# One operation moved from VectorE into ScalarE's root, and a new order of all engines, in a recurrent block on one core

## The chip, the cores and the metric

The kernel runs on one core of a Trainium2 chip. The metric is the time of one execution in device microseconds, from the first to the last work of the core. The engines are TensorE (PE: matmuls; PEld is its weight load), VectorE (DVE), ScalarE (ACT), GpSimd (POOL) and SyncE (SP), which issues most of the transfers. Each works through its own list in order and waits on semaphores for the others.

## The reference

The input `x` has 8 sequences of 1024 tokens with 256 channels, in float32. The block normalizes each token and adds two branches to it:

```python
xn = _layernorm(x)
x = x + hawk(xn) + ffn(xn)

# hawk: 384 hidden channels
gate = einsum('bsd,hd->bsh', xn, Wg);  u = einsum('bsd,hd->bsh', xn, Wi)
y = causal_conv4(u, conv_w) + conv_b                    # per channel
ig = sigmoid(einsum('bsh,gh->bsg', y, lru_Wi) + lru_bi)
rg = sigmoid(einsum('bsh,gh->bsg', y, lru_Wg) + lru_bg)
alpha = exp(-8.0 * softplus(lam) * rg)
beta = sqrt(1.0 - alpha ** 2 + 1e-06)
xbeta = beta * ig * y
h[t] = alpha[t] * h[t-1] + xbeta[t]                     # a scan over the tokens
hawk = einsum('bsh,dh->bsd', gelu(gate) * h, Wo)

# ffn: a token mix, then
r = sigmoid(xr @ W_r);  k = square(relu(xk @ W_k));  ffn = r * (k @ W_v)
```

`xr` and `xk` mix each token with the one before it, by channel.

## The kernel before

The kernel goes through the 8 sequences one after the other; a hidden tile is `[128 channels, 3 chunks m, 1024 tokens]`, so an operation on one chunk is 128x1024, and a half is 512 tokens (L or R). All data is float32.

Most of the products are done by a scheme that saves one in eight: `Group` (L569) makes a 2x2 block product of seven products (11 for `o`), from sums of weight blocks (`weight_sum`, POOL, once at the start) and sums of token halves (`token_sum`, POOL, L1024). Its steps are named after the family: `u0`, `u1`, `u2` (the 768 outputs of `Wi` and `Wg`), `k`, `r`, `v` and `o`. `k mm 0` to `k mm 6` are the seven products (PE; `product` at L533, two matmul instructions of 128x512 each, or `product_by_token` at L539, eight of 128x128); `seed` copies bank A to a new bank B and `five` bank C to SBUF (ACT, L589, L593); `fork_c` and `fork_d` add B to what was copied (DVE, L596, L605); `evict` and `late` take results out. Product 0 goes to bank A, which `seed` must copy before product 2 (by token: 3) adds to it. Product 4 adds the token sum 1 of the family, which is made by `token_sum k 2`. In the first sequence `u0` is made by plain products instead, in four quarters of the tokens for each of two blocks (`u0_0 quarter`, L668, four instructions of 128x256), so that work can begin with the first tokens; its input `xnT` comes by PE transposes and four copies (`early_put`, ACT, L1246).

The gates `rg` and `ig` use a 3x3 scheme with 15 products each (`rg p11`, ...), from sums of halves of `y` (`form`, DVE, L816) and of weights (`gate_weight`, POOL, L858, once). `keep` and `copy` are copies of banks (ACT, L727, L724), `join` adds a bank and a kept half (DVE, L735), and `evict` takes the tanh of a bank into `tr` (for `rg`) or `ti` (for `ig`) (ACT, L739). A sigmoid is made of the tanh of half the argument, so that a factor 0.5 is left over for later.

The steps around the change work on one chunk `m`:

- `decay(m)` (ACT, L1135): `tr` becomes a = exp(rate * tr + rate). `rate` comes from the parameters by small steps `constant 0` to `constant 18`, the last of them at L498 on DVE.
- `decay_square(m)` (ACT, L1138): `q` = a a.
- `decay_rest(m)` (DVE, L1141): `q` = 1 - a a.
- `beta(m)` (ACT, L1144): `q` = sqrt(q + 1e-6).
- `gated_input(m)` (DVE, L1148): `ti` = (ti + 1) * y; `scaled_input(m)` (DVE, L1151): `ti` = 0.5 * ti * q.
- `recur(m)` (DVE, L1156): the scan, by halves; `gated_state` (DVE, L1160): gelu(gate) times the state, which the products with `Wo` read (`o mm`, and for the last sequence `own o_product` and `own o_tile`, L1051).

In the sequences 0 to 6 `decay`, `decay_square` and `decay_rest` stand in the sequence's own part of the order and the rest in the next one's; the last sequence does all of it for itself (`own ...`). Other steps that are named below: `normalize` (ACT, L970, for the sequence after), `deviation` (its root, L953), `stats` (DVE, L946, L950), `mix_before` and `mix` (ACT, L1035, and DVE, L1041: the token mix), `add_x` (a transfer issued by POOL that adds `x` to the output tile, L1078), `halve v` (POOL, L514).

ScalarE holds the tables of a set of functions at a time. The trace shows a load (ACT_TABLE_LOAD) before the root, the exponential, the tanh and the gelu when another kind came before; exp and tanh share a set, gelu and tanh as well.

The order of every engine is written out: `at(f, ...)` adds a step under its name, with the position that `PLACES` holds for that name ("first", "second", "middle" and "last" sequence) plus the sequence's entry of `BASES`. At the end all steps are sorted by position and issued, each on its engine. The positions are in the unit of microseconds, but only their order has an effect; data dependences and semaphores follow from the order.

Of the kernel before, what the change touches and what calls it, by code (L numbers as in the profile page):

```python
# [9 lines left out]
AF = mybir.ActivationFunctionType  # L10
ALU = mybir.AluOpType
# [7 lines left out]
BETA_EPS = 1e-6  # L19
# [17 lines left out]
        "early_transposes 1": -8.6439, "u0_0 quarter 1 0": -8.0543, "early weight_sum u 2": -3.8020,  # L37
        "early_put 1": -3.0538, "early normalize 4 1": -0.3355, "early weight_sum k 0": -0.0898,
        "early weight_sum k 1": -0.0893, "early weight_sum r 2": -0.0060,
        "early weight_sum k 2": 0.6225, "early deviation 6 2": 0.8567, "early weight_sum r 0": 1.1454,  # L40
        "early normalize_on_vector 5": 1.2994, "u0_0 quarter 0 0": 1.2999, "early_transposes 2": 1.2999,
        "u0_0 quarter 0 1": 1.3004, "early inverse 6 2": 1.4202, "early normalize_on_vector 7": 1.4207,
        "early normalize 6 1": 1.4212, "early gate_weight 18": 1.5352, "early weight_sum u 0": 1.7246,
        "early weight_sum u 1": 1.7251, "early_put 2": 1.7885, "early gate_weight 0": 1.8328,
        "early parameters": 1.9171, "early_transposes 3": 1.9259, "early_put 3": 1.9264,
        "early mix_before k 1": 1.9269, "u1 mm 0": 3.1720, "early token_sum x 0": 3.5163,
        "u0_0 quarter 1 1": 3.5290, "early weight_sum u 3": 3.6691, "u2 mm 0": 3.7112,
        "early mix k 1": 3.8314, "early constant 0": 4.0632, "early token_sum x 1": 4.4256,
        "early mix_before k 0": 5.9712, "early mix k 0": 6.0616, "early load 0 8": 7.4642,
        "early mix_before r 0": 8.3295, "early mix r 0": 8.3300, "u2 seed": 8.6340,  # L50
        "u0_0 evict 1 0": 8.7097, "u0_0 evict 0 0": 8.7413, "early token_sum x 2": 9.4143,
        "early token_sum k 0": 10.1772, "second stats 5 1": 10.6110, "early token_sum r 0": 10.8667,
        "second stats 4 1": 11.3491, "u0_0 quarter 1 2": 11.4875, "u0_0 quarter 1 3": 11.4879,
        "u0_0 evict 1 1": 11.4885, "u2 mm 1": 11.8761, "u1 mm 1": 12.0652, "second stats 1 1": 12.2744,
        "early token_sum k 1": 12.2953, "u1 seed": 12.3010, "u2 five": 12.6356,
        "early constant 1": 12.6580, "u1 mm 2": 13.0964, "u1 evict A 0 0": 13.0969,
        "early constant 2": 13.2671, "second stats 3 1": 13.9558, "second stats 6 1": 13.9907,
        "u2 mm 3": 14.2992, "conv_first 1": 14.5919, "second stats 7 1": 14.6574,
        "second stats 2 1": 15.0552, "early weight_sum k 3": 15.5297, "second stats 0 1": 15.5372,
        "conv_rest 1 1": 15.5372, "u2 mm 2": 16.0627, "early mix_before r 1": 16.3697,  # L60
        "k mm 0": 16.3737, "k seed": 16.3742, "k mm 2": 16.3747, "k mm 1": 16.4858,
        "k evict A 0 0": 16.4931, "u0_0 quarter 0 2": 16.8650, "early token_sum k 3": 16.9641,
        "k five": 17.1660, "early constant 3": 17.1999, "conv_rest 1 2": 17.7117, "deviation": 17.8286,
        "u0_0 quarter 0 3": 18.2151, "early token_sum k 2": 18.5156, "k mm 3": 19.5026,
        "k fork_c": 20.0768, "early constant 4": 20.1410, "early constant 5": 20.1415,
        "early constant 6": 20.1420, "u0_0 evict 0 1": 20.2772, "u2 evict A 0 0": 20.2868,
        "early halve v": 20.6806, "inverse 0 8": 21.3608, "normalize 1 1": 21.3613,
        "early constant 7": 21.5110, "early mix r 1": 21.5785, "early weight_sum r 1": 22.0990,
        "normalize 6 1": 22.6887, "r mm 0": 23.1799, "r seed": 23.1804, "k mm 4": 23.9848,
        "r mm 3": 24.1395, "k fork_d": 24.1400, "early constant 8": 24.1585, "u2 fork_c": 24.2562,  # L70
        "u1 mm 3": 24.5089, "normalize 7 1": 24.8151, "u1 five": 24.9788,
        "early token_sum r 1": 25.1316, "r evict A 0 0": 25.2098, "conv_first 0": 25.4504,
        "normalize 2 1": 25.4982, "early gate_weight 11": 25.6372, "k mm 5": 25.7409,
        "early token_sum r 2": 26.1668, "k mm 6": 26.1955, "r mm 2": 26.1986, "r mm 1": 26.6667,
        "conv_rest 1 3": 27.0060, "conv_rest 0 1": 28.4200, "u1 fork_c": 28.6675,
        "conv_rest 0 2": 28.9892, "u1 mm 4": 29.5016, "u1 mm 5": 29.5176, "k evict B 1 0": 29.6818,
        "k evict C 0 1": 29.6820, "k square 0": 29.6823, "normalize 5 1": 29.8290, "r five": 29.8586,
        "u1 evict C 0 1": 30.1053, "u2 mm 5": 30.8282, "normalize 4 1": 30.9791,
        "transposes 1 1": 30.9796, "early token_sum x 3": 30.9835, "k late": 31.4107,
        "early constant 9": 31.9860, "early weight_sum v 0": 32.0816, "u1 fork_d": 32.0871,  # L80
        "r fork_c": 32.0872, "early constant 10": 32.0935, "conv_rest 0 3": 32.0938,
        "early constant 11": 32.0940, "early weight_sum o 0": 32.1222, "early gate_weight 17": 32.3477,
        "r mm 4": 33.0834, "form 0": 33.3300, "form 1": 33.3305, "u2 mm 4": 33.8429,
        "v_product 0": 33.8429, "early weight_sum r 3": 34.1459, "transposes 0 1": 34.1807,
        "normalize 0 1": 34.3885, "k square 1": 35.0468, "conv_first 2": 35.0517,
        "u2 evict C 0 1": 35.0972, "put_transposed 1 1": 35.1766, "u1 mm 6": 35.7392,
        "early gate_weight 19": 36.6572, "v_product 4": 37.0114, "conv_rest 2 1": 37.0336,
        "early gate_weight 2": 37.1069, "early token_sum r 3": 37.4370, "r fork_d": 37.5271,
        "r late": 37.5276, "early constant 12": 37.5345, "u2 fork_d": 37.7650, "u2 mm 6": 38.3899,
        "r mm 6": 38.4971, "conv_rest 2 2": 38.6946, "early constant 13": 39.4021,  # L90
        "early gate_weight 7": 39.4190, "conv_rest 2 3": 39.4739, "early gate_weight 1": 39.4739,
        "early gate_weight 12": 39.4744, "put_transposed 0 1": 39.6428, "u1 evict B 1 0": 39.6492,
        "normalize 3 1": 39.6727, "transposes 1 0": 39.6732, "put_transposed 1 0": 39.6737,
        "r mm 5": 39.6869, "form 2": 39.7379, "early weight_sum v 2": 39.7441,
        "early gate_weight 4": 39.8463, "early gate_weight 8": 40.0476, "transposes 0 0": 40.1660,
        "put_transposed 0 0": 40.4633, "v_product 2": 40.7467, "r evict C 0 1": 40.8812,
        "u2 evict B 1 0": 40.9052, "u1 late": 40.9351, "r evict B 1 0": 41.0098, "form 3": 41.2098,
        "form 4": 43.0821, "ig p11": 43.0826, "rg p11": 43.7513, "load_for_squares": 44.8161,
        "rg copy B": 45.3918, "v_product 6": 45.3923, "rg p0": 45.3923, "token_sum x 0": 45.7012,
        "value 4": 45.7514, "rg p4": 46.4712, "value 2": 46.7711, "early gate_weight 5": 46.9214,  # L100
        "form 8": 47.2752, "early gate_weight 13": 47.3300, "form 5": 48.1910, "ig copy B": 48.2529,
        "mix_before r 1": 48.2544, "rg keep 14": 48.2575, "rg keep 10": 48.7892,
        "early gate_weight 9": 49.4059, "early gate_weight 10": 49.7857, "ig p4": 50.0465,
        "ig keep 10": 50.2130, "early gate_weight 15": 50.5880, "mix_before k 0": 50.5982,
        "form 6": 51.2676, "value 6": 51.6062, "form 7": 51.6063, "early gate_weight 6": 51.9650,
        "form 9": 52.1153, "stats 2 1": 52.1945, "mix_before r 0": 53.6127, "ig p0": 53.8491,
        "rg p3": 53.9727, "stats 6 1": 54.4985, "stats 4 1": 54.5807, "mix_before k 1": 54.6938,
        "rg p10": 55.4065, "early gate_weight 16": 55.5289, "ig p3": 55.6292, "ig keep 14": 55.8307,
        "ig p10": 55.8312, "rg keep 13": 55.8456, "rg p7": 55.9304, "mix r 0": 55.9576,
        "early constant 14": 56.1814, "early gate_weight 14": 56.5499, "rg copy E": 57.4426,  # L110
        "ig keep 13": 57.6010, "rg join G": 57.9749, "rg p2": 57.9754, "rg keep 8": 57.9834,
# [1350 lines left out]
```

## Time and profile before

| | us |
| --- | --- |
| median of 3 runs (lowest to highest) | 621.52 (620.99 to 622.68) |
| profiled execution, its time | 621.6 |
| its span, first to last instruction | 619.8 |
| busy: PE, DVE, ACT, POOL | 598.8, 569.1, 489.7, 281.9 |
| L1141 on DVE, 24 instructions | 19.1 |
| L1144 on ACT, 24 roots | 27.5 |
| table loads on ACT, 39, each | 1.28 |

The granted TensorE clock is 1.00 throughout. Busy times of PE count each matmul to its modelled end, and matmuls that follow each other overlap: in a steady run two instructions of 128x512 take 0.86 us, and one of them is listed with 0.595. So PE's idle time, not its busy share, tells what is to be had.

### The profile page before, as it was taken

Reading aid. Unit: us, or ns where it says so; the run is one execution under the profiler, and the core shown is the slowest. Engines: PE = TensorE matmul, PEld = TensorE weight load, DVE = VectorE, ACT = ScalarE, POOL = GpSimd, SP = SyncE. Lnnn points to the kernel's source line nnn. Section 1 sums busy time; section 2 is a strip of 40 time slices with the busy share of each in tenths; the row PEclk is TensorE's granted clock in tenths of the full one; section 3 lists DMA queues with packets and bytes.
Section 4 is the critical chain, followed back from the end, with each engine's and each line's share of the span. In section 5 each row is a group of like instructions: output and inputs, shape, how many; then the busy total and the mean of one; then the engine's idle time right before and its main releaser. Section 6 shows DMA issues by size and latency. Waiting matters only on the chain.

```text
span 619.8 us, 7495 instructions
## 1 busy us (share of the span) xinstructions
PE 598.8 (97%) x2491; PEld 358.6 (58%) x2491; DVE 569.1 (92%) x772; ACT 489.7 (79%) x730; POOL 281.9 (45%) x205
## 2 busy tenths in 40 slices
PE   8888999999999999999999999999999999999997
PEld 4456434684357844586446954569445774555576
DVE  5999889998999988999899998999989997798896
ACT  4985799928998489974999479993899839995890
POOL 4998592245616363362823546154552618110010
PEclk9999999999999999999999999999999999999999
DMA  7203004053300434017040250403430020400053
GB/s 272 68 2 69 1 0 68 0 113 92 55 13 3 122 81 68 1 27 175 4 69 2 61 143 6 63 0 98 106 55 14 22 82 33 68 2 1 0 85 120
DMA packets 35478, 35.10 MB, mean 57 GB/s; under 512 B 2800, under 2 KB 34928, under 8 KB 35440
## 3 DMA queue, kind: packets, MB, share of 16 engines
q1 hardware_dynamic: 26416, 25.63, 15.4%
q0 software_dynamic: 8320, 8.39, 9.1%
q10 hardware_dynamic: 704, 0.60, 0.3%
q8 instruction: 20, 0.33, 0.2%
q14 instruction: 18, 0.15, 0.1%
HBM read 19.94 MB, written 8.39 MB: 46 GB/s over the span
## 4 chain that ended last, share of the span: by engine, by line
PE 72%; DVE 16%; ACT 8%; issue 3%; POOL 1%; DVEq 0%; ACTq 0%; POOLq 0%
PE bank L533 52%; PE bank L539 17%; DVE y L1124 5%; PE bank L1051 2%; DVE xk L1041 1%; DVE bank L596 1%; PE bank L1214 1%; DVE u L816 1%; POOL q L1024 1%; DVE xk L1001 1%; ACT q L1144 1%; ACT xk L1035 1%; POOL xsum L1024 1%; DVE side L914 1%; ACT bank L724 1%
## 5 line engine op out<-in xcount | busy, mean ns | idle before, releaser
L1124 DVE SCALAR_TENSOR_TENSOR y<-u,par,y 128x1024 f32<-128x1024 f32 x72 | 96.3, 1360 | 0.8 <-ACT y L1115 0.7
L533 PE MATMUL bank<-u,gate_w 128*128 128x512 f32 x192 | 92.6, 595 | 1.8 <-ACT side L896 1.0
L533 PE MATMUL bank<-y,gate_w 128*128 128x512 f32 x160 | 78.7, 595 | 1.1 <-ACT bank L724 1.1
L533 PE MATMUL bank<-xsum,sum_u 128*128 128x512 f32 x138 | 69.8, 597 | 1.3 <-DVE bank L596 1.2
L533 PE MATMUL bank<-ysum,gate_w 128*128 128x512 f32 x128 | 64.8, 595 | 2.1 <-ACT ti L727 1.6
L533 PEld LDWEIGHTS bank<-u,gate_w 128*128 128x128 f32 x192 | 34.9, 189 | 42.1 <-issue 32.9
L533 PEld LDWEIGHTS bank<-y,gate_w 128*128 128x128 f32 x160 | 29.7, 189 | 39.9 <-issue 28.2
L1035 ACT ACTIVATE xk<-xnT,mu_rest 128x1024 f32<-128x1024 f32 x16 | 18.4, 1148 | 41.6 <-DMA xnT<-xk 24.6
L1024 POOL TENSOR_TENSOR xsum<-xnT 128x512 f32<-128x512 f32 x16 | 22.7, 1433 | 56.7 <-DMA xnT<-xk 32.1
L533 PE MATMUL bank<-xnT,w_u 128*128 128x512 f32 x92 | 47.1, 593 | 0.5 <-ACT bank L589 0.5
L1024 POOL TENSOR_TENSOR q<-g 128x512 f32<-128x512 f32 x12 | 20.1, 1672 | 60.2 <-DVE g L1160 60.2
L724 ACT COPY bank<-bank 128x512 f32<-128x512 f32 x48 | 27.8, 582 | 23.8 <-PE bank L533 20.0
L1024 POOL TENSOR_TENSOR q<-g,q 128x512 f32<-128x512 f32 x12 | 25.3, 2104 | 46.1 <-DVE g L1160 30.5
L533 PEld LDWEIGHTS bank<-ysum,gate_w 128*128 128x128 f32 x128 | 23.7, 189 | 34.0 <-issue 19.5
L596 DVE TENSOR_TENSOR bank<-bank,five 128x512 f32<-128x512 f32 x52 | 35.0, 688 | 6.5 <-PE bank L539 4.3
L533 PEld LDWEIGHTS bank<-xsum,sum_u 128*128 128x128 f32 x138 | 24.1, 190 | 26.9 <-issue 19.4
L593 ACT COPY five<-bank 128x512 f32<-128x512 f32 x52 | 30.7, 590 | 10.1 <-PE bank L539 9.5
L970 ACT ACTIVATE xt<-xt,mv,std 128x256 f32<-128x256 f32 x60 | 35.2, 597 | 2.3 <-DVE mv L961 2.3
L539 PE MATMUL bank<-w_o,g 128*128 128x128 f32 x288 | 36.9, 275 | 0.0
L539 PEld LDWEIGHTS bank<-w_o,g 128*128 128x128 f32 x288 | 35.0, 192 | 2.9 <-issue 2.9
L1151 DVE SCALAR_TENSOR_TENSOR ti<-ti,q 128x1024 f32<-128x1024 f32 (+1 forms) x25 | 29.3, 1173 | 3.4 <-ACT q L1144 3.3
L589 ACT COPY bank<-bank 128x512 f32<-128x512 f32 x52 | 30.6, 589 | 2.2 <-PE bank L539 1.3
(187 smaller groups left out, 1589.1 us busy)
## 6 DMA issues: line engine op xcount, KB each, us to landing
side<-in_x_dram POOLq DMA_DIRECT2D x8, 1024.0 KB, 9.4
xt<-in_x_dram SPq DMA_DIRECT2D x28, 256.0 KB, 4.9
xnT<-xk SPq DMA_DIRECT2D x96, 64.0 KB, 2.0
out_dram<-side SPq DMA_DIRECT2D x12, 512.0 KB, 3.3
xt<-in_x_dram SPq DMA_DIRECT2D x1, 1024.0 KB, 5.6
out_dram<-side SPq DMA_DIRECT2D x4, 256.0 KB, 2.2
out_dram<-side SPq DMA_DIRECT2D x6, 128.0 KB, 1.8
q<-in_lru_wg_dram SPq DMA_DIRECT2D x1, 576.0 KB, 6.1
```

Of the source, the lines that this page charges most:

```text
L533: nc.tensor.matmul(banks[b], weight, tokens, start=start, stop=True, skip_group_check=True)
L539: nc.tensor.matmul(banks[b][:, p], tokens[:, p], weight, start=start and j == 0, stop=True, skip_group_check=True,)
L589: nc.scalar.copy(banks[bank["B"]], banks[bank["A"]])
L593: nc.scalar.copy(held["five"], banks[bank["C"]])
L596: nc.vector.tensor_tensor(banks[bank["C"]], banks[bank["B"]], held["five"], ALU.add)
L724: nc.scalar.copy(banks[bank[new]], banks[bank[key]])
L970: nc.scalar.activation(xa, xa, AF.Identity, bias=m, scale=r)
L1024: nc.gpsimd.tensor_tensor(dst[o], a, b, ALU.subtract)
L1035: nc.scalar.activation(mixes[which][:, c, :], xnT[:, c, X0 - 1 : X0 - 1 + S], AF.Copy, scale=mu_rest[:, n : n + 1])
L1051: nc.tensor.matmul(banks[b][:, j * D : (j + 1) * D], lhs[:, c, (t + j) * P : (t + j + 1) * P], families[w][:, c, :], start=(j == 0 and c = ...
L1124: nc.vector.scalar_tensor_tensor(y[:, m, :], u[:, m, k : k + S], column(COL_CONV_W + k * HC + m), y[:, m, :], ALU.mult, ALU.add,)
L1151: nc.vector.scalar_tensor_tensor(ti[:, m, p], ti[:, m, p], 0.5, q[:, m, p], ALU.mult, ALU.mult)
```

## The change

`decay_rest` goes, 24 instructions on DVE. `beta` takes a a itself: its scale is -(10^6)/2^20 and its bias (10^6 + 1)/2^20, which makes it sqrt((1 + 1e-6 - a a) * 10^6/2^20), that is the root of before times 1000/1024. `scaled_input` takes 0.512 for 0.5, which makes up for it. `PLACES` and `BASES` are new as a whole (the names are the same but for `decay_rest`), so every engine has a new order in all sequences.

```diff
-BETA_EPS = 1e-6
...
-BASES = [9.828, 71.0849, 152.108, 224.215, 296.322, 368.429, 440.537, 512.644]
+BASES = [10.9113, 57.2608, 149.2927, 221.3999, 293.5071, 365.6143, 437.7215, 511.5455]
...
-    beta_eps = fixed("beta_eps", [1])
+    beta_one = fixed("beta_one", [1])
...
-    def decay_rest(m):
-        nc.vector.tensor_scalar(q[:, m, :], q[:, m, :], -1.0, 1.0, ALU.mult, ALU.add)
-
     def beta(m):
-        nc.scalar.activation(q[:, m, :], q[:, m, :], AF.Sqrt, bias=beta_eps)
+
+        nc.scalar.activation(q[:, m, :], q[:, m, :], AF.Sqrt, bias=beta_one, scale=-(10**6) / 2**20)
...
     def scaled_input(m, p=slice(0, S)):
-        nc.vector.scalar_tensor_tensor(ti[:, m, p], ti[:, m, p], 0.5, q[:, m, p], ALU.mult, ALU.mult)
+        nc.vector.scalar_tensor_tensor(ti[:, m, p], ti[:, m, p], 0.512, q[:, m, p], ALU.mult, ALU.mult)
...
-        nc.gpsimd.memset(beta_eps, BETA_EPS)
+        nc.gpsimd.memset(beta_one, (10**6 + 1) / 2**20)
...
                 at(decay_square, m)
-                at(decay_rest, m)
```

The tables of positions are long; these are the stretches of the orders that they give which the prediction speaks of ("x 2" is `token_sum x 2`, "ws u 0" is `weight_sum u 0`, "q 1 0" is `u0_0 quarter 1 0`):

| | before | after |
| --- | --- | --- |
| PE, first sequence, from the second transposes | transposes 1, q 1 0, q 0 0, transposes 2, q 0 1, transposes 3, u1 mm 0, q 1 1, u2 mm 0, q 1 2, q 1 3, u2 mm 1, u1 mm 1, u1 mm 2, u2 mm 3, u2 mm 2, k mm 0, k mm 2, k mm 1, q 0 2, q 0 3, k mm 3, r mm 0, k mm 4, r mm 3, u1 mm 3, k mm 5, k mm 6, r mm 2, r mm 1 | q 0 0, q 1 0, transposes 1, 2, 3, q 1 2, q 0 2, q 0 3, q 1 1, q 0 1, u1 mm 1, u2 mm 0, q 1 3, u1 mm 0, k mm 0, u1 mm 3, u2 mm 2, k mm 1, u1 mm 2, u2 mm 3, k mm 2, u1 mm 5, r mm 0, u2 mm 1, k mm 3, u1 mm 4, u2 mm 4, u2 mm 5, transposes 1 0 (next sequence), u1 mm 6, k mm 4, k mm 5, r mm 1, r mm 3 |
| POOL, first sequence | ws u 2, k 0, k 1, r 2, k 2, r 0, u 0, u 1, gate_weight 0, x 0, ws u 3, x 1, x 2, k 0, r 0, k 1, ws k 3, k 3, k 2, halve v | ws u 0, u 2, r 0, u 1, r 2, k 2, r 1, k 0, gate_weight 1, 17, x 2, x 0, x 1, x 3, k 0, ws u 3, k 1, ws k 1, ws r 3, r 0, ws k 3, halve v, r 1, k 3, k 2, r 2 |
| ACT, first sequence | constant 1 (Exp), ..., deviation (root), u0_0 evict, u2 evict A (gelu), two normalize, r seed | deviation (root), u1 evict A, constant 1 (Exp), ..., u2 evict A (gelu), r seed |
| ACT, end of the first sequence | decay 0, rg copy F, decay_square 0, ig evict E, ig keep 8, ig copy F | rg copy F, ig keep 8, u0 five, ig evict G, ig copy F, decay 0, decay_square 0 |
| ACT, end of the last sequence | own beta 1, rg evict A, ig evict A, own decay 2, own decay_square 2, ig evict F, own beta 2 | own beta 1, rg evict A, ig evict A, own decay 2, own decay_square 2, own beta 2, ig evict F |
| DVE, end of the last sequence | gated_input 2 L, decay_rest 2, gated_input 2 R, ..., then behind the root: scaled_input 2 L, recur 2 L, gated_state 2 L, scaled_input 2 R, add_hawk 4, recur 2 R, add_hawk 2, gated_state 2 R | gated_input 2 L, ..., then behind the root: scaled_input 2 L, recur 2 L, gated_state 2 L, gated_input 2 R, scaled_input 2 R, recur 2 R, gated_state 2 R, add_hawk 4 |

## The prediction

> **What bounds the kernel now.** I read the busy times first, then the same by stage, then the waits of PE in the timeline, then the last 25 us on ACT and DVE.
>
> ```profile
> PE 598.8 (97%) x2491; PEld 358.6 (58%) x2491; DVE 569.1 (92%) x772; ACT 489.7 (79%) x730; POOL 281.9 (45%) x205
> ```
>
> ```profile
> 0.00:30.00 30.00, 25.06 (x86) 13.83 (x87) 22.60 (x55) 20.20 (x33) 21.61 (x29) 1.00 0.51 175
> 30.00:81.00 51.00, 45.05 (x170) 25.80 (x169) 45.48 (x66) 37.59 (x60) 39.75 (x37) 1.00 0.10 22
> 81.00:153.00 72.00, 68.61 (x306) 41.97 (x305) 67.61 (x87) 56.49 (x87) 32.87 (x23) 1.00 0.27 59
> 225.00:297.00 72.00, 71.47 (x314) 43.30 (x313) 68.48 (x89) 58.25 (x88) 32.06 (x21) 1.00 0.27 59
> 560.00:620.00 60.00, 54.94 (x213) 35.54 (x211) 49.90 (x68) 37.06 (x50) 4.08 (x3) 1.00 0.23 53
> ```
>
> The columns are the window, its length, then busy time and count on PE, PEld, DVE, ACT and POOL. PE is the bound: no matmul is added or removed, so only its idle time can be won, 21 us of the span in all. Of it 4.9 + 6.0 lie before 81 us and 3.4 in the second sequence; from 153 to 560 the windows add up to 1.8 us; the last window has 5.1, mostly behind the last matmul. So DVE's 92% hides behind PE almost everywhere, and the question is what the new order does at the two ends.
>
> ```profile
> 26.03 1.13 PE L533 MATMUL bank<-xk,w_k 128*128 128x512 f32 x2 [1.45 <-ACT bank L589]
> ...
> 34.80 1.16 PE L539 MATMUL bank<-w_r,xr 128*128 128x128 f32 x8 [1.62 <-ACT bank L589]
> ...
> 79.41 1.98 PE L533 MATMUL bank<-y,gate_w 128*128 128x512 f32 x4 [1.14 <-ACT bank L724]
> ...
> 168.85 1.10 PE L533 MATMUL bank<-xsum,sum_u 128*128 128x512 f32 x2 [0.42 <-DVE bank L596]
> ...
> 607.83 8.90 PE L1051 MATMUL bank<-w_o,g 128*128 128x256 f32 x40 [1.07 <-DVE g L1160]
> ```
>
> In brackets stands PE's idle time before each row and what ended it.
>
> **The step that goes.**
>
> ```profile
> L1141 DVE TENSOR_SCALAR q<-q 128x1024 f32<-128x1024 f32 x24 | 19.1, 798 | 2.6 <-ACT q L1138 1.9
> ```
>
> 24 instructions, 19.1 us of DVE, 2.0 to 2.8 per sequence. The median is 692 ns; one took 3.22 us:
>
> ```profile
> 162.96 1.54 POOL L1078 DMA_DIRECT2D side<-in_x_dram  x1
> ...
> 163.15 3.82 DVE L1141 TENSOR_SCALAR q<-q 128x1024 f32<-128x1024 f32 x2
> ```
>
> It stood beside POOL's issue of the `add_x` transfer; DVE came 2.5 us late to `u0 fork_c`, and PE waited the 0.42 us shown at 168.85. That goes: -0.4 (none if the new order puts another wait there; -1.1 if the 0.7 us that the waits give to the same line in the second sequence went too). Elsewhere PE's work hides the step; in the steady stretch I take -0.3 of the 1.8 us idle. The bounds are -1.8, and +2.0 if the new order opens waits there (153 to 225 has 0.95 idle, the next window 0.53: 0.4 more in each of five sequences). The cover that makes these 17 us worth nothing is PE itself.
> The Trainium skill ("SBUF — State Buffer", on the shared port pair) says that a one-source VectorE operation in a two-port mode and a GpSimd operation exclude each other for a whole instruction. The long row fits. By that rule every removed step would also free POOL, by an estimate 24 x 0.69 = 17 us, and the sum would be the same as long as POOL, 45% busy, isn't what PE waits for; the trace shows one long step in 24, and I count one.
>
> **What ScalarE takes on.** Nothing in number: the root has a bias from a tile already (24 x 1150 ns); the scale is a constant. Bounds: 1150 and, with a scale from a tile too, `decay`'s 1252; I take 1150, the same function and shape. The high end would put 3 x 0.10 = 0.3 us on the tail, the rest is hidden.
>
> **The start.** Here the order decides. Take a matmul step of 128x512 as a piece of 0.86 us (two instructions; the chain of waits has 34 of them in 14.68 us at 139.24). PE had done 14 pieces behind the transposes (6 quarters of `u0_0`, 8 steps) at 24.4, then waited 1.45: `k mm 2` stands right behind `k mm 0` and needs `k seed` on ACT. At 34.80 `r mm 3` waits for `r seed`, behind two table loads on ACT (28.66 and 30.74, 1.28 each). In the new list five steps stand between `k mm 0` and `k mm 2`, ten between `r mm 0` and `r mm 3`, and the Exp of `constant 1` comes after `deviation`, so one of the table loads goes. Both waits go. What is late next? POOL:
>
> ```profile
> 17.26 2.27 POOL L1024 TENSOR_TENSOR xsum<-xnT,xsum 128x512 f32<-128x512 f32 x1
> ...
> 28.00 2.25 POOL L1024 TENSOR_TENSOR xk<-xk 128x512 f32<-128x512 f32 x1
> ```
>
> The second row is `token_sum k 2`, done at 30.2; `k mm 4` needs it. In the new queue of POOL there stand ahead of and with it, from 8.34 on: three wide and five narrow weight sums and two gate weights (3 x 1.0 + 5 x 0.46 + 2 x 0.75 = 6.8, to 15.1), ten token sums, four more weight sums and `halve v` (1.0 + 3 x 0.45 + 2.47 = 4.8). The eight token sums from 15.05 to 30.25 took 1.26 to 2.27, mean 1.76: `k 2` ends at 15.1 + 17.6 + 4.8 = 37.5 (32.6 with all at 1.27, 42.4 with all at 2.25). PE on its side: the transposed input is whole at 14.4 (the four copies follow each other on ACT; before, 15.0), five quarters to 18.7, then seven pieces, 14 done at 24.7, then 11 pieces, `r mm 0` (0.9) and a transpose step (0.45) to 35.5. So `k mm 4` starts at 37.5, POOL the later. Before, as much was done at 39.9 (the thirteenth piece after the fourteen ended at 40.3; less 0.4, as one of mine is a transpose). The term is 37.5 - 39.9 = -2.4, from -4.4 (PE ready at 35.5 sets it) to +2.5 (42.4). I take the mean row, since both kinds come in the same stretch.
>
> **The decay rate.**
>
> ```profile
> 76.34 1.28 ACT L1135 ACT_TABLE_LOAD   x1 [1.70 <-DVE rate L498]
> ```
>
> `decay 0` waited for the last of the small constants on DVE, with two copies of the gate banks queued behind it on ACT; PE's 1.14 at 79.41 is that. In the new list `decay 0` comes behind these copies. What PE then meets isn't shown: 0 to -1.1, I take half, -0.5. The other waits up to 168 us (0.5 to 1.5 each, on ACT, DVE and POOL) I leave as they are: they are as likely to move as to go.
>
> **The tail.**
>
> ```profile
> 601.93 0.67 ACT L739 ACTIVATE ti<-bank,half_b 128x512 f32<-128x512 f32 x1
> 602.62 1.28 ACT L1144 ACT_TABLE_LOAD   x1
> 603.92 1.15 ACT L1144 ACTIVATE q<-q,beta_eps 128x1024 f32<-128x1024 f32 x1
> ...
> 602.06 0.69 DVE L1141 TENSOR_SCALAR q<-q 128x1024 f32<-128x1024 f32 x1
> ...
> 605.10 0.69 DVE L1151 SCALAR_TENSOR_TENSOR ti<-ti,q 128x512 f32<-128x512 f32 x1 [0.54 <-ACT q L1144]
> ```
>
> ACT runs without a gap from 576.6 to 605.1 and sets the last root. The removed step at 602.06 ended at 602.75, inside the table load: worth nothing. But the new list puts `ig evict F` (first row) behind the last root, which so comes 0.6 us earlier. Its price: one more table load (1.28) and the tanh (0.67) behind the root, 1.95, beside DVE's left half (scale 0.69, scan 1.22, gate 0.69 = 2.6); then `gated_input 2 R` (0.67) joins DVE's right half: 0.67 + 0.68 + 1.28 + 0.68 = 3.3 against PE's 16 matmuls x 0.216 = 3.5. Both fit, by 0.65 and 0.2. Gain -0.6, at most the 1.07 that PE waits; +0.7 if the right half isn't covered.
> Against this move speaks the Trainium skill ("ScalarE: Activation LUTs", What ACT_TABLE_LOAD costs), with about 2.66 us per switch, a drain included. The trace shows 1.28 to the start of the root; by the page's figure the left half would no longer cover load and tanh (an estimate: 3.3 against 2.6), and 0.7 would be lost.
>
> **Sum.** -0.4 - 0.3 - 2.4 - 0.5 - 0.6 = -4.2, from the profiled execution's 621.6 (span 619.8 and 1.8 around it): 617.4. The median of the runs is 621.52, so nothing has to be moved. All best ends together: -0.4 -0.7 (the 1.1) - 1.8 - 4.4 - 1.1 - 1.1 = -9.5; all worst: +2.0 + 0.3 + 2.5 + 0.7 = +5.5.
>
> **Rivals.** (1) Slower: POOL's queue in the start. If its token sums run at 2.25 each, against DVE's `mix` and statistics, `k mm 4` starts at 42.4, PE is 2.5 behind the old order, and being full from then on it never makes that up: 624.1 if nothing else is won. It hurts from an end of `k 2` at 39.9, and is visible from 41.8. For it: four of eight sums took 2.2 or more, and POOL is 72% and 78% busy in the first windows. Against: that all ten do. (2) No change: PE has a floor, and what is won at the start is met again by a wait in the second sequence (3.4 us there): 621.6, within 1.9. For it: the steady stretch leaves nothing. (3) The change as forecast, but `beta` slower by a tenth: adds 0.3, inside the range.
>
> **Chances.** About 0.3% (1.9 us) is what a measurement of this kernel can tell from no change: faster is below 619.7, slower above 623.4. Forecast 0.55, rival 1 0.24, rival 2 0.21. The likeliest case alone spans 613.0 to 619.6. The range reaches up to rival 1's 624.0 and down to 613.0, where three of the five terms are at their better ends; what lies beyond either end takes several bounds at once.
>
> **What would show it.** L1141 gone and DVE near 550 us busy; no table load ahead of `deviation` in the first 30 us; PE's row of `k mm 4` between 35.5 and 39.9, released by POOL; the windows from 153 to 560 as full as now; the last root ahead of a tanh, PE's last wait under 0.6. Wrong: a wait on POOL over 4 us at about 40; PE idle in a steady sequence; more than 1 us of PE idle inside the last o products.

## The result: slower, and where the time went

| | before | after |
| --- | --- | --- |
| median of 4 runs (lowest to highest), us | 621.51 (620.99 to 622.68) | 651.07 (648.72 to 652.10) |
| ratio, with its 95% interval | | 1.0471 [1.0454, 1.0489] |
| profiled execution, its span, us | 621.6, 619.8 | 650.6, 648.8 |
| mean granted clock of TensorE | 1.00 | 0.98 |

The changed kernel is slower by 29.6 us, or 4.7%. The page of the profile, first its busy times, then the granted clock in 40 slices of 16.2 us:

```profile
PE 611.0 (94%) x2491; PEld 362.0 (56%) x2491; DVE 581.7 (90%) x748; ACT 493.3 (76%) x730; POOL 275.0 (42%) x205
...
PEclk9999999999999989999799998999979999899999
```

DVE lost its 24 instructions (772 to 748) and 19.1 us of work with them, and yet it is busy for 12.6 us longer. A digit below 9 in the last line is a dip of the clock; there is one per sequence from the third to the seventh. The same windows as before (window, length, busy and count on PE, PEld, DVE, ACT and POOL, granted clock, DMA share, GB/s):

```profile
0.00:30.00 30.00, 25.99 (x87) 14.00 (x88) 22.04 (x56) 20.42 (x34) 22.23 (x30) 1.00 0.52 176
30.00:81.00 51.00, 48.54 (x180) 27.34 (x179) 47.31 (x68) 38.99 (x64) 41.78 (x35) 1.00 0.24 42
81.00:153.00 72.00, 70.07 (x308) 42.20 (x307) 69.40 (x90) 59.81 (x89) 33.83 (x26) 1.00 0.17 44
225.00:297.00 72.00, 66.34 (x298) 40.94 (x297) 67.36 (x79) 53.09 (x80) 29.09 (x19) 0.98 0.25 52
297.00:370.00 73.00, 68.10 (x300) 41.76 (x299) 65.99 (x81) 54.70 (x82) 29.53 (x20) 0.95 0.23 47
```

Up to 153 us the new order is the better one: PE is busy for 5.9 us longer than before in the first three windows, so more has been done. From 225 to 514 us each window lacks PE work: 298 matmuls instead of 314 in the first of them. What PE waited for there (waits of PE: total us, times, longest):

```profile
PE bank L529 <- DVE bank L731: 19.6, 7, 4.7
PE bank L529 <- DVE bank L592: 6.5, 8, 1.9
```

Line 731 is `join` on DVE; before, PE waited 0.5 us for it in the whole run. One such wait in the timeline of PE, at 318.81 in the fourth sequence:

```profile
313.11 1.02 PE L529 MATMUL bank<-xsum,sum_u 128*128 128x512 f32 x2
318.81 2.07 PE L529 MATMUL bank<-ysum,gate_w 128*128 128x512 f32 x2 [4.68 <-DVE bank L731]
320.67 1.92 PE L529 MATMUL bank<-u,gate_w 128*128 128x512 f32 x2
```

PE stands still for 4.68 us, and then two pairs of matmuls take 2.07 and 1.92 us in place of 1.02. What DVE did meanwhile:

```profile
310.29 7.31 DVE L1142 SCALAR_TENSOR_TENSOR ti<-ti,y 128x1024 f32<-128x1024 f32 x1
...
318.08 0.67 DVE L731 TENSOR_TENSOR bank<-bank,ti 128x512 f32<-128x512 f32 x1
```

This is `gated_input 0`, one instruction, which took 1.2 us before (1212 ns by its median) and whose median is still 1219 ns. The join that PE waits for stands behind it in DVE's queue. And POOL in the same stretch:

```profile
310.01 1.55 POOL L1074 DMA_DIRECT2D side<-in_x_dram  x1
310.97 1.89 POOL L1020 TENSOR_TENSOR xk<-xk 128x512 f32<-128x512 f32 x1
312.20 1.89 POOL L1020 TENSOR_TENSOR xsum<-xnT,xsum 128x512 f32<-128x512 f32 x1
313.43 1.87 POOL L1020 TENSOR_TENSOR side<-xk,side 128x512 f32<-128x512 f32 x1
314.66 1.86 POOL L1020 TENSOR_TENSOR xr<-xr 128x512 f32<-128x512 f32 x1
```

`add_x` is issued at 310.01, with four token sums queued behind it. `gated_input 0` begins 0.28 us later and ends at 317.60, 1.1 us after the last sum (314.66 + 1.86 = 316.52): about as long as it needs for itself (1.22). So it looks as if it got nothing done while the sums lasted. The same happens behind each of the six issues from the second sequence to the seventh: 3.82 us at 156.40 (three sums), 7.31 or 7.32 at 229.72, 310.29, 390.84 and 471.12 (four sums each), 4.86 at 553.64 (it began when the second of four sums was running). Each time it ends 1.1 us after the last queued sum.

Before, from the third sequence on, `add_x` had no sum close behind it, since the old list put it after the sums `x 3`, `k 3` and `k 2`. In the new list it moved from position 95.49 of a steady sequence to 75.20, past them, and `r 2` of the next sequence stands behind it as the fourth. For comparison the kernel before:

```profile
311.62 1.84 POOL L1078 DMA_DIRECT2D side<-in_x_dram  x1 [1.41 <-DVE side L907]
...
311.24 1.22 DVE L1148 SCALAR_TENSOR_TENSOR ti<-ti,y 128x1024 f32<-128x1024 f32 x1
312.38 0.69 DVE L1141 TENSOR_SCALAR q<-q 128x1024 f32<-128x1024 f32 x1
```

Those are rows of the kernel before, POOL and DVE: `gated_input` overlaps with the issue there as well and takes its 1.22 us, and `decay_rest`, which begins 0.76 us behind the start of the issue, takes its 0.69. The issue alone holds nothing up.

**The account.** I added up PE's matmuls in order of time at their steady pitch (0.429 us for 128x512, 0.216 for 128x256, 0.112 for 128x128) and noted when the same amount of work was done in each kernel:

| work done, us of PE | before | after | e1 | e9 | e11 |
| --- | --- | --- | --- | --- | --- |
| 80 | 93.24 | 89.25 | 89.21 | 88.94 | 89.93 |
| 160 | 179.33 | 173.95 | 173.76 | 172.75 | 177.88 |
| 300 | 320.99 | 330.26 | 316.37 | 314.94 | 320.05 |
| 500 | 522.84 | 547.56 | 521.05 | 516.24 | 521.32 |
| 585 | 610.68 | 639.68 | 609.57 | 604.09 | 609.16 |

(e1, e9 and e11 are experiments told below.) After leads by 5.4 us at 160 and is 29.0 behind at the end, so 34.4 are lost on the way. Between two issues of `add_x` in the steady stretch there are 80.4 us on average (third to seventh sequence), against 73.2 before. Of these 7.2 us, 4.7 are the wait for the join and 2.2 the slow matmuls behind it: 1.8, 2.8, 1.8 and 2.6 us in the four sequences (the seven matmuls from 318.81 on took 5.8 us to the start of the next one, and 7 x 0.43 = 3.0 is their pitch). The remaining 0.3 is other waits.

### The profile page after: what moved, and what is told of

Same layout as the page of the kernel before. It is cut to its first block, busy times and chain, and to the rows that moved or that the text cites. A ratio compares the mean times of both kernels' runs of the same rounds, so it can differ in the third digit from the quotient of the medians.

```text
span 648.8 us, 7410 instructions
## 1 busy us (share of the span) xinstructions
PE 611.0 (94%) x2491; PEld 362.0 (56%) x2491; DVE 581.7 (90%) x748; ACT 493.3 (76%) x730; POOL 275.0 (42%) x205
## 4 chain that ended last, share of the span: by engine, by line
PE 61%; DVE 21%; ACT 13%; issue 3%; DMA 1%; SPq 0%; DVEq 0%; ACTq 0%
PE bank L529 37%; PE bank L535 20%; DVE ti L1142 6%; DVE q L1150 3%; DVE ti L1145 2%; DVE y L1120 2%; PE bank L1047 2%; ACT tr L1131 2%; DVE bank L731 1%; ACT tr L735 1%; ACT q L1134 1%; DVE bank L592 1%; ACT q L1138 1%; DVE g L1154 1%; ACT ti L735 1%
## 5 line engine op out<-in xcount | busy, mean ns | idle before, releaser
L1120 DVE SCALAR_TENSOR_TENSOR y<-u,par,y 128x1024 f32<-128x1024 f32 x72 | 100.3, 1402 | 0.4 <-ACT y L1111 0.2
L529 PE MATMUL bank<-u,gate_w 128*128 128x512 f32 x192 | 95.7, 615 | 1.4 <-ACT bank L720 1.3
L529 PE MATMUL bank<-ysum,gate_w 128*128 128x512 f32 x128 | 69.8, 631 | 19.5 <-DVE bank L731 19.4
L529 PE MATMUL bank<-xsum,sum_u 128*128 128x512 f32 x138 | 71.2, 616 | 3.6 <-DVE bank L592 3.3
L1142 DVE SCALAR_TENSOR_TENSOR ti<-ti,y 128x1024 f32<-128x1024 f32 (+1 forms) x25 | 60.6, 2427 | 4.3 <-ACT ti L735 4.3
L529 PEld LDWEIGHTS bank<-xsum,sum_u 128*128 128x128 f32 x138 | 26.4, 201 | 35.3 <-issue 26.8
L892 ACT ACTIVATE side<-bank 128x512 f32<-128x512 f32 x24 | 14.2, 598 | 32.8 <-PE bank L535 32.4
L592 DVE TENSOR_TENSOR bank<-bank,five 128x512 f32<-128x512 f32 x52 | 34.8, 687 | 3.4 <-PE bank L529 1.7
L1020 POOL TENSOR_TENSOR q<-g,q 128x512 f32<-128x512 f32 x12 | 23.9, 1995 | 30.3 <-DVE g L1154 30.3
L1020 POOL TENSOR_TENSOR xsum<-ysum 128x512 f32<-128x512 f32 x12 | 16.4, 1371 | 43.1 <-ACT ysum L878 39.3
```

Of the source, the lines that this page charges most:

```text
L529: nc.tensor.matmul(banks[b], weight, tokens, start=start, stop=True, skip_group_check=True)
L592: nc.vector.tensor_tensor(banks[bank["C"]], banks[bank["B"]], held["five"], ALU.add)
L892: nc.scalar.activation(dst, src, AF.Tanh, scale=0.5)
L1020: nc.gpsimd.tensor_tensor(dst[o], a, b, ALU.subtract)
L1120: nc.vector.scalar_tensor_tensor(y[:, m, :], u[:, m, k : k + S], column(COL_CONV_W + k * HC + m), y[:, m, :], ALU.mult, ALU.add,)
L1142: nc.vector.scalar_tensor_tensor(ti[:, m, p], ti[:, m, p], 1.0, y[:, m, p], ALU.add, ALU.mult)
```

## The experiments

Three theories were set against each other. A: the issue of a POOL transfer ahead of queued token sums shuts DVE out until the last of them is done, and the fix is to put it behind them. B: the new order of the steady sequences is too tight in itself, and the long instruction is only where it shows. C: the clock falls first, for whatever reason, and the waits follow. Ratios are to the kernel before, run on the same chip, with 95% intervals.

| | what it is | us | ratio |
| --- | --- | --- | --- |
| e1 | after, `add_x` behind the sums | 620.47 | 0.9986 [0.9975, 0.9997] |
| e2 | after, no `add_x` in sequences 1 to 6 | 621.09 | 0.9991 [0.9979, 1.0004] |
| e3 | before, `add_x` ahead of three sums | 647.37 | 1.0415 [1.0383, 1.0446] |
| e4 | before's order, new root alone | 620.28 | 0.9975 [0.9965, 0.9985] |
| e5 | after, `gated_input 0` behind the sums | 625.59 | 1.0059 [1.0037, 1.0080] |
| e6, e10 | e1, old root and `decay_rest` back | 638.86, 640.88 | 1.0289 [1.0259, 1.0319], 1.0311 [1.0290, 1.0331] |
| e7, e9 | start of after, the rest in before's order, new root | 615.51, 616.29 | 0.9900 [0.9885, 0.9915], 0.9919 [0.9905, 0.9932] |
| e8 | e1, `ig evict F` ahead of the last root | 621.90 | 1.0006 [0.9991, 1.0022] |
| e11 | e9, old root and `decay_rest` back | 621.31 | 1.0004 [0.9995, 1.0013] |

### What holds DVE up: e1, e2, e3, e5

**e1**: the changed kernel with `add_x` alone moved back.

```diff
+PLACES["second"]["add_x"] = 104.5
+PLACES["middle"]["add_x"] = 83.9
```

> The changed kernel, with one step moved: add_x of the sequences 1 to 6 stands on POOL behind the token sums that it stood ahead of. Theory A (POOL's transfer issue, with four token sums queued behind it, shuts DVE's next operation of two SBUF inputs out until the last of them is done): no gated_input over 2.5 us, PE's waits of 4.7 us gone, clock 1.00; the lead of 5.7 us that PE has at equal work of 200 us stays, so 615 to 618. Theory B (the new order of PE and DVE in the steady sequences is itself too tight, whatever POOL does): over 640. Theory C (the clock of TensorE falls first and everything follows): clock under 1.00 and over 630.

Measured: 620.47 us, 30.6 less than the changed kernel; the granted clock is 1.00, no `gated_input` takes over 2.12 us, and DVE is busy for 557.6 us. One position undoes the loss. C falls with this, since nothing was done to TensorE. In the changed kernel the order was the reverse of C as well: in the trace's clock records the half clock of the fourth sequence starts at 317.4, 3.3 us into the wait that began at 314.13. The number is 2 to 5 us above what was expected, though, and B has to answer for that. PE in e1, one row of several of the kind, and its waits:

```profile
246.34 1.12 PE L531 MATMUL bank<-xnT,sum_u 128*128 128x512 f32 x2 [0.96 <-DVE bank L594]
```

```profile
PE bank L531 <- DVE bank L594: 7.1, 7, 1.4
```

The step is a `fork` that stands in DVE's queue behind the long instructions of the recurrence. The table above shows the lead of 5.6 us at 160 shrink to 1.8 at 500, by 3.8 in the 340 us between, or 0.8 per sequence. So B is right in a small way: the new steady order, with `add_x` mended, gives back nearly all that the new start wins.

**e2**: `add_x` taken out of sequences 1 to 6 (so the residual `x` is missing in their output), the sums left where they are.

```diff
-            at(add_x, s)
+            if first or last:
+                at(add_x, s)
```

> The changed kernel without add_x in the sequences 1 to 6, so the residual is missing in their outputs; the token sums stay where they are. Theory A1 (it takes the transfer's issue ahead of the sums): gated_input at about 1.2 to 2.3 us, time 614 to 618. Theory A2 (four token sums in a row on POOL starve a DVE operation of two SBUF inputs by themselves): gated_input still at 5 us or more, time over 640. Theory B: over 640 with gated_input short.

Measured: 621.09 us. All runs of `gated_input` in e2 (least, median and longest in ns, first and last start):

```profile
L1142 DVE SCALAR_TENSOR_TENSOR ti<-ti,y x25: 683/1221/2100, 84.9 to 608.3; 128x1024 f32<-128x1024 f32 x23, 128x512 f32<-128x512 f32 x2
```

The longest is now 2.10 us, beside seven sums in a row:

```profile
305.67 1.27 POOL L1020 TENSOR_TENSOR xk<-xk 128x512 f32<-128x512 f32 x1
306.90 2.26 POOL L1020 TENSOR_TENSOR xsum<-xnT,xsum 128x512 f32<-128x512 f32 x1
...
305.92 2.10 DVE L1142 SCALAR_TENSOR_TENSOR ti<-ti,y 128x1024 f32<-128x1024 f32 x1
```

Here `gated_input` ends 1.1 us after the one sum that was running when it began, and the next sum takes 2.26 us instead of 1.27: the two engines take turns. So the sums without the transfer delay DVE by 0.9 us at most; it takes the issue ahead of them to shut it out for 6.1, and then the whole row of sums goes first. That the transfer's own traffic of 1.0 MB doesn't matter is shown by e1, which has all of it.

**e3**: the reverse, in the kernel before. Its `add_x` is put ahead of the last three sums.

```diff
+PLACES["middle"]["add_x"] = 82.19
```

> The kernel before, with one step moved: add_x of the sequences 2 to 6 stands ahead of the last three token sums instead of behind them. Theory A: the next DVE operation with two SBUF inputs or in the one-input form of L1141 takes about 1 + 3 x 1.23 + its own 0.7 to 1.2, 4.5 to 6 us, and each of the five sequences loses 2 to 4 us: 631 to 641. Theory B: no loss, 621 to 623.

Measured: 647.37 us, above the expected stretch: one position of one step makes the old kernel slower by 25.9 us. POOL and DVE in e3:

```profile
317.54 1.56 POOL L1079 DMA_DIRECT2D side<-in_x_dram  x1 [5.14 <-DVE side L908]
318.49 1.92 POOL L1025 TENSOR_TENSOR xsum<-xnT,xsum 128x512 f32<-128x512 f32 x1
319.73 1.90 POOL L1025 TENSOR_TENSOR side<-xk,side 128x512 f32<-128x512 f32 x1
320.95 1.89 POOL L1025 TENSOR_TENSOR xk<-xk 128x512 f32<-128x512 f32 x1
...
317.16 1.22 DVE L1149 SCALAR_TENSOR_TENSOR ti<-ti,y 128x1024 f32<-128x1024 f32 x1
318.30 5.11 DVE L1142 TENSOR_SCALAR q<-q 128x1024 f32<-128x1024 f32 x1
```

Here the `gated_input` began before the issue and was spared, and the one shut out is the instruction behind it, `decay_rest`, which has a single input. It took 5.11 us in place of 0.69 and ended 0.57 after the last sum. So it isn't `gated_input` alone, and it isn't the new root: it is the order on POOL.

**e5**: the changed kernel with `add_x` left ahead of the sums, and `gated_input 0` moved behind them on DVE's side.

```diff
+PLACES["middle"]["gated_input 0"] = 10.09
```

> The changed kernel with add_x where the change put it, but in the middle sequences gated_input 0 (two SBUF inputs) stands on DVE behind the statistics and joins that read PSUM or one input, next to gated_input 1. If it takes a two-input DVE operation to be shut out, and the operations of one input or of PSUM run beside POOL's four sums freely: no gated_input over 2.5 us in the sequences 2 to 6, no PE wait over 2 us there, 619 to 623 (the one block of 4.9 us in the last sequence stays). If POOL's stretch holds up DVE whatever it does: over 640.

Measured: 625.59 us, 25.5 less than the changed kernel. DVE in e5 beside the issue at 304.88 and the four sums behind it (to 311.43):

```profile
305.15 0.42 DVE L943 BATCH_NORM_STATS2 st<-xt 128x6 f32<-128x256 f32 x1
...
307.39 0.70 DVE L732 TENSOR_TENSOR bank<-bank,ti 128x512 f32<-128x512 f32 x1 [1.60 <-PE bank L530]
...
311.29 1.23 DVE L1143 SCALAR_TENSOR_TENSOR ti<-ti,y 128x1024 f32<-128x1024 f32 x1
```

Joins (one input from a bank, one from SBUF) and statistics (one input) run in that stretch at their usual 0.70 and 0.42 us. Of what these runs put beside such a stretch, `gated_input` (two inputs from SBUF) and the TENSOR_SCALARs (`decay_rest`, and a small constant in the first sequence) are shut out. One block of 4.84 us is left in e5, at 529.66, where the list of the last sequence holds and nothing was moved; its slow matmuls cost 1.8 us, and PE's waits on the `fork` are 10.4 us in 8, against 7.1 in 7 in e1.

Taken together, A holds: the block follows `add_x` (e1, e2), can be made in the old kernel (e3), and can be dodged from DVE's side (e5). What stays open is why the exclusion lasts over several of POOL's instructions when a transfer was issued ahead of them, and not otherwise. The rows show one difference: behind an issue each sum is listed as starting about 0.65 us before the one ahead of it ends, and without it the sums follow each other almost without overlap. Whether that keeps DVE from its turn isn't tested. The transfer is issued by POOL in all of these kernels; one issued by another engine in its place wasn't tried.

### What the root and the new order are worth: e4, e6, e10

**e4**: the kernel before, its order kept, with `decay_rest` gone and the new constants of the root.

```diff
-                at(decay_rest, m)
...
-        nc.scalar.activation(q[:, m, :], q[:, m, :], AF.Sqrt, bias=beta_eps)
+        nc.scalar.activation(q[:, m, :], q[:, m, :], AF.Sqrt, bias=beta_one, scale=-(10**6) / 2**20)
```

> The kernel before in its own order, with decay_rest gone, the new scale and bias of the root and the factor 0.512. By the prediction's two terms for this part (the long step beside add_x in the first sequences, and the steady stretch): -0.7, so 620.8. If the step was hidden entirely: 621.5. If DVE's relief was worth more than PE's waits show: under 619.

Measured: 620.28 us, a ratio of 0.9975: 1.5 us (0.9 to 2.2), twice the 0.7 that the prediction's two terms for it come to. In an order that was laid out for the step, its removal is worth next to nothing, as PE covers it. The second sequence of e4 shows more, POOL and DVE:

```profile
162.17 1.54 POOL L1077 DMA_DIRECT2D side<-in_x_dram  x1
163.12 1.89 POOL L1023 TENSOR_TENSOR side<-xk,side 128x512 f32<-128x512 f32 x1
...
162.36 3.75 DVE L1144 SCALAR_TENSOR_TENSOR ti<-ti,y 128x1024 f32<-128x1024 f32 x1
```

`decay_rest` is gone, and the next instruction in the queue, `gated_input`, is held in its place: 3.75 us, to 1.1 us after the sum.

**e6 and e10**: e1 with the step and the old root put back, in e6 about 3 us ahead of each root, in e10 2.5 us behind each square (in e6, `decay_rest 1` of sequence 6 comes behind its root, so that this root takes the square itself).

```diff
+PLACES["first"]["decay_rest 0"] = ...
...
+PLACES["last"]["own decay_rest 2"] = ...
```

> The kernel e1_add_late with decay_rest and the old root put back: the new order alone, without the change of arithmetic. If the two parts add up (root only -1.4 in the old order, e1 -1.2 in all): 621 to 623. If the new order lives from the freed DVE: over 625. DVE busy about 17 us more than in e1.

> The order of the change with add_x behind the sums and the old root, decay_rest now placed 2.5 behind its decay_square instead of shortly ahead of the root as in e6. If e6 lost its time to the place of decay_rest: 621 to 624. If the new steady order has no room for 2.1 us more of DVE per sequence: over 627.

Measured: 638.86 and 640.88 us, 18 and 20 above e1, with two different places for the step. From the second sequence's `add_x` (166.50) on, no instruction of DVE in e10 is longer than 2.3 us, so it isn't A again. PE's waits in e10:

```profile
PE bank L544 <- DVE bank L607: 15.6, 7, 2.6
PE bank L1062 <- DVE g L1172: 4.1, 1, 4.1
```

The same `fork` as in e1, and now 2.2 us at a time: the new order has spent the 2 us of DVE per sequence that the step leaves free. Of the 20 us between e10 and e1, 13.4 are more idle time of PE and 6.7 slow matmuls behind its longest waits (by the pitch above; the mean granted clock of e10 is 0.989). The step costs 1.5 us in the old order and 18 to 20 in the new one. What a step is worth depends on the order around it, and both numbers are right.

### What the start is worth: e7, e9, e11

**e7 and e9**: the new order for the first two sequences, with `add_x` of the second behind its sums, the old order for the other six, the new root everywhere. In e7, at the seam of the two orders, one `gated_input 2` comes ahead of the `ig evict A` whose result it should take; e9 moves that one step.

```diff
+PLACES["second"]["add_x"] = 104.5
+PLACES["second"]["ig evict A"] = 112.0
+PLACES["middle"] = ... (as before, without decay_rest)
+PLACES["last"] = ... (as before, without decay_rest)
```

> The new root, the new order for the first and the second sequence, the old order (without decay_rest) for the others, add_x of the second behind its sums. PE's lead at equal work of 160 us was 5.4 in e1, and the old steady order lost less per sequence (0.5 to 1.0 of idle against 1.5). If both hold across the seam: 614 to 617, under both kernels. If the seam opens waits: 618 to 622.

> e7_mixed with one position mended at the seam (ig evict A of the second sequence comes ahead of gated_input 2, which reads what it writes). The two parts as before: the new order for the first two sequences, the old one for the rest, the new root: 615 to 616, PE's lead at equal work of 160 us about 5.5 and kept to the end. If e7 was fast only by the step in the wrong place: 618 or more.

Measured: 615.51 and 616.29 us. e9 is faster than the kernel before by 0.8% and than the changed one by 34.8 us. In the profiled execution (615.06, the fastest of five; by the medians e9 is 4.9 ahead of its own runs of the kernel before) it has a lead of 6.6 us at 160 and the same at 585. So the old steady order opens no waits of its own. Its busy times:

```profile
PE 598.7 (98%) x2491; PEld 357.4 (58%) x2491; DVE 552.7 (90%) x748; ACT 489.3 (80%) x729; POOL 280.2 (46%) x205
```

**e11**: e9 with the old root and `decay_rest` back.

> e9_mixed with the old root and decay_rest put back: of the whole change only the new order of the first two sequences is left. By equal work the new start led by 5.4 to 5.8 at 160 us, of which the freed DVE had some 1.1 by e4: 616 to 618. If the start's gain hangs on the freed DVE: over 619.

Measured: 621.31 us, no different from before, and 5.0 above e9. Its lead is 3.3 us at 80 and 1.4 at 160: between 81 and 153 us PE idles for 8.0 us (by the same pitch), against 3.7 in e9, and 4.1 of it are waits for DVE (two for a `join`, one for a `fork`) where e9 waits for DVE for 0.8 at a `fork` and hardly elsewhere. So the start and the freed DVE pay together (5.0 us) and much less apart (nothing in e11, 1.5 in e4): with the three steps still on DVE, the second sequence eats the lead.

### The tail: e8

**e8**: e1 with `ig evict F` put ahead of the last root again, as it was before.

```diff
+PLACES["last"]["ig evict F"] = 77.38815
```

> The kernel e1_add_late with ig evict F of the last sequence ahead of the last root again, as in the kernel before. By the prediction's term for the tail this gives back 0.6: about 621.1, PE's wait ahead of the last 40 matmuls 2.3 in place of 1.68, one table load fewer. If the order there does nothing: 620.5.

Measured: 621.90 us, where e1 has 620.47 in another set of runs; in the two profiles 585 us of PE's work are done at 610.5 and 609.6, and 0.4 of these 0.9 us are there at 500 already. PE's last wait in e8 (total us, times, longest), and the row behind the same wait in e1:

```profile
PE bank L1050 <- DVE g L1157: 2.3, 1, 2.3
```

```profile
606.72 8.90 PE L1049 MATMUL bank<-w_o,g 128*128 128x256 f32 x40 [1.68 <-DVE g L1156]
```

2.3 against 1.68: the move is worth 0.6 us of wait, and in e1 the 40 matmuls behind it follow each other without a gap.

## Why the prediction was wrong, by its own steps

**The step that failed: a move that was never costed.** The part-by-part section costs the removed step, the start, the decay rate and the tail. In the steady stretch it costs nothing but the removed step, and for the new order it writes "+2.0 if the new order opens waits there", worked out from one small wait of the old kernel. It doesn't name `add_x` among the steps that are moved past others, though `add_x` is a transfer issue on POOL and moved past three token sums. What the steady order was priced at, +2.0 at worst, came to +34.4 us from the point of 160 us on. The move of `add_x` decides the sign: without it (e1) the kernel takes 620.47 us. "PE idle in a steady sequence" stood among the prediction's own signs of being wrong, and it is what came.

**The row was there.** The prediction shows L1141 at 3.22 us "beside POOL's issue of the `add_x` transfer", and books it as a gain, because L1141 goes. Its reading was one step short: the row shows the partner too. In that one sequence of the old kernel (the second) one token sum stood behind `add_x`, at 163.92 for 1.89 us, so to 165.81; the long L1141 ended 0.6 us later (0.69 is its own time), the second of the pair 1.2 us later. ("2.0 to 2.8 per sequence" misses this: the three steps of that sequence come to 4.6 us.) In the third and all later sequences of before no sum stood close behind it, and no instruction there was long. Removing the victim doesn't remove the cause: e4 shows the next instruction as the victim, at 3.75 us. The price could have been read there too: one queued sum cost 2.5 us, and the four of the new list 6.1.

**The rule that was weighed.** The prediction drew on the Trainium skill ("SBUF — State Buffer", Who interferes with whom) for an exclusion that lasts for one instruction, with "the sum would be the same" either way. The page also says that a VectorE instruction with two inputs in SBUF contends with a GpSimd instruction that reads SBUF, and one with at most one such input, outside the two-port modes, does not; e5's joins and e1's and e2's `gated_input` (2.12 and 2.10 us at most, a wait for one sum) agree. What no instruction-by-instruction rule gives is 7.31 us for 1.22 us of work behind an issue; here the measurement decides.

**The steady windows** were to be "as full as now"; the one to 225 us was, and in each of the four from 225 to 514 PE idles for 4.9 to 5.7 us. And even in e1 they are not as full: about 0.8 us per sequence, 3.8 from 160 to 500, against the 2.0 of the bound.

**The start** was right in sign and too small. The account has 5.4 us of lead at 160, where -0.4 - 2.4 - 0.5 were forecast. Its inner step of POOL held:

```profile
35.30 1.13 PE L529 MATMUL bank<-xsum,sum_u 128*128 128x512 f32 x2 [1.39 <-DVE bank L592]
...
38.42 1.88 PE L529 MATMUL bank<-xk,sum_k 128*128 128x512 f32 x4
```

`token_sum k 2` ended at 37.9 (forecast 37.5, in POOL's row of 2.25 us at 35.65); the forecast start of `k mm 4` was 37.5, and it came at 38.42: 1.5 us ahead of the 39.9 of before, where 2.4 was forecast. PE, not POOL, was the later by then, through 1.39 us on DVE at 35.30, a wait that the forecast doesn't have. No table load stands ahead of `deviation`, as forecast. What was mis-sized is the rest, "left as they are": PE's waits of 0.2 us or more between 40 and 81 us were 4.0 before, with the 1.14 of the decay rate among them, and are 0.9 after, and between 81 and 153 us PE's idle time by the pitch fell from 4.6 to 3.7.

**The removed step** was forecast at -0.7 in all and is -1.5 alone (e4). By equal work e4 leads by 1.1 us at 160, the end that the prediction gave as its better one: the wait of 0.42 at 168.85 is down to 0.1, and the 0.74 at the `fork` at 102.8 is gone. That the two pay 3.5 more together than apart (5.0 - 1.5 - 0) isn't in the sum, since the sum adds parts that don't add.

**The tail**: -0.6 forecast, 0.6 of wait shown by e8. But PE's last wait was to be under 0.6 and is 1.7 in the changed kernel and 1.68 in e1. In e1 PE arrived earlier than before (605.04, against 606.76), and the last root, behind ACT's own chain, only 1.1 us earlier (603.95 against 605.07). A chain that is bound by ACT doesn't follow PE's lead. The root itself is 1.15 us, as taken, and one table load 1.28; in e1 the tanh starts 1.32 us after the root's end (603.95) and is done at 605.95, 0.6 ahead of `gated_input 2 R` at 606.58. The figure of about 2.66 us in the Trainium skill ("ScalarE: Activation LUTs", What ACT_TABLE_LOAD costs) would have cost 0.7 by the prediction's estimate, and no run shows it.

**The rivals.** Rival 1 was the right family, a POOL queue, in the wrong place: it looked at how late POOL would be in the start, and the harm came from what POOL does to DVE in the steady stretch. Rival 2 described e11 and, nearly, e1.

## What to carry to other kernels

When an order is laid out anew, list every step that changed its neighbours on each queue, and price DMA issues on POOL first: in this kernel `add_x` belongs behind POOL's queued sums (e1), and where it stands ahead of them DVE did best with only joins and statistics beside it (e5). A single odd duration in a trace is worth its partner: ask what stood beside and behind it on the other engine, and whether the change makes that more common. And a removed step has no price of its own: here it was worth 1.5 us in the old order, 18 to 20 in the new one, and 5 with the new start.

## What was not expected of the hardware

- In these runs `gated_input` (two inputs from SBUF) or a TENSOR_SCALAR that begins while sums stand queued behind POOL's issue of a transfer is held until the last of the queued sums is done: `gated_input` takes 3.82 us beside three sums and 7.31 beside four, where 1.22 is its own time. Without the issue the longest is 2.10 beside seven sums (e2). In the first sequence of the changed kernel, at 67.97, a small constant (`constant`, L492 on DVE) was held for 2.9 us, to 70.91; the last of the two sums behind the issue ended at 70.88.
- Sums behind the issue are listed with 1.86 to 1.92 us and start 1.23 us apart; in e1, ahead of the issue, most are listed with 1.27 and start as far apart. The listed time there overlaps, and the rate of POOL doesn't change.
- After 4.68 us without a matmul the next two pairs took 2.07 and 1.92 us, twice the usual, and the granted clock of the window from 297 to 370 us was 0.95. That cost 2.8 us on top of the wait. The clock records of the changed kernel have five stretches at half the clock before its end, three of 3.4 and two of 6.8 us, and each begins inside such a wait or at most 0.7 us behind it. Shorter waits did it at times: in e5 1.86 us, with the next pairs at 1.41, 1.91 and 1.63, and in e10 two of four waits of 2.64 to 2.65, with pairs of up to 2.08; those of 1.3 us in e5 did not. "TensorE: Matmul & The Clock Gate" (Part 1) in the Trainium skill gives half the clock after at least one idle window of about 3.4 us. The half agrees with the rows; as a least length of the wait the 3.4 us don't hold here.
